# First feed-forward of a two-layer decoder: the scratch of the Hadamard transform laid out by token tile

## The chip, the cores and the metric

The kernel runs on one core of one Trainium2 chip. The metric is the device time of the launch in microseconds (us). Most times below come from one profiled execution, which is described with its own time.

The engines have the names that the profile gives them: PE is TensorE (matrix products, with its weight loads apart as PEld), DVE is VectorE, ACT is ScalarE, POOL is GpSimd, and SP is SyncE, whose queue issues nearly all transfers (DMAs).

## The reference

The program is a decoder of two layers on x of shape (4, 512, 512), four batches of 512 tokens with 512 features. Each layer has a self-attention, a cross-attention and a feed-forward, and each of these six phases ends with `x = layernorm(x + phase(x))`. The change is in the first layer's feed-forward, which works with quantised activations and ternary weights:

```python
def act_quant(x, bits=8):                      # per token
    qb = 128.0
    scale = qb / clip(max(abs(x), axis=-1), 1e-5)
    return clip(round(x * scale), -qb, qb - 1) / scale

def weight_quant(w):                           # ternary
    scale = 1.0 / clip(mean(abs(w)), 1e-5)
    return clip(round(w * scale), -1, 1) / scale

bitlinear = lambda x, w: act_quant(x) @ weight_quant(w).T
gate, up = bitlinear(x, w_gate), bitlinear(x, w_up)       # 512 -> 2048
intermediate = silu(gate) * up
y = bitlinear(fwht(intermediate), w_down)                 # 2048 -> 512
```

`fwht` is the normalised Walsh-Hadamard transform over the 2048 features of a token. It mixes all 2048 features, and the quantisation after it needs the largest magnitude over all 2048 of a token.

## The kernel before

**Phases and lanes.** The phases are called A to F, and each is a Python generator that runs once for each batch: A0 to A3, then B0 to B3, and so on. The first feed-forward is phase C, in `l0_ffn`. The function `lanes` keeps at most two of these tasks alive and advances them in turn, so that C1's first half is recorded between the steps of C0's second half; C2 is alive beside C1's end, and C3 beside C2's second half. Work in the background (loading and quantising weights) is advanced beside them. Inside a task, `Pipe` delays a step by so many ticks. Each engine executes its own instructions in the order that results from this.

**Buffers.** Nearly all tiles are 128 partitions x 2 KB. They come from two pools in SBUF (69 tiles called "o", 13 called "t") and from 8 banks of PSUM.

**Phase C, first half.** Activations are feature-major here: the 512 tokens of the batch lie along a tile's row, 128 features along the partitions. For each of 16 feature tiles o, four products into `pg` (L645) and four into `pu` (L647) give gate and up; DVE, ACT and POOL form silu(gate) * up and split it in two parts (L616 to L624). The transform is factored in two, 2048 = 16 x 128. The factor of 128 is a product with a 128 x 128 matrix `had` over the partitions (L629 and L630, called `ph`). ACT copies the result to a tile `hw` (L635), and SP writes it to a DRAM scratch (L636): 128 rows of 2 KB, one for each feature, in the place o * 128 of a (2048, 512) array. There are two such scratches, used by even and odd batches.

**The way back.** The factor of 16 runs over features that lie in different tiles o. So the scratch is read back (L652) as 16 tiles `z`, tile c holding features i * 128 + c * 8 + b for all 16 i and 8 b, with all 512 tokens in a row. A partition is a pair (i, b), a row is 2 KB, and eight rows that touch stand 256 KB apart from the next eight.

**Phase C, second half.** Now the result is wanted token-major. For each token tile i of 128 tokens and each group g of four, a pass of four products (L713, out `had`, in the profile's name) takes the 128 columns of token tile i out of z tiles 4g to 4g + 3 as weights, against `had16`, and fills a PSUM bank with 512 transformed features of 128 tokens. There are 16 passes for a batch, in the order i = 0, g = 0..3, then i = 1, and so on. A product of f32 appears as two instructions, so a pass is eight of them.

After a pass, `amax` takes the largest magnitude (DVE, L659) and copies the bank out as `q2f` (ACT, L661). After the four passes of a token tile, `scales` forms the scale (L666 to L671), `quant` rounds (ACT L679, DVE L680), `turn` transposes the result back to feature-major by eight products for each half (L686, `q2T`), `flip` copies it (ACT L691), `down` multiplies it with the 16 row tiles of w_down (L699, `dn`), and `add` adds the residual and takes the statistics for the layer norm (L703, L176). In C1 and C3 TensorE's queue holds the passes among transposes and down products of the batch before.

**Weights.** `layout` prepares the inputs on the host, before the launch. It permutes the 2048 rows of w_down to the order in which the passes leave the features.

## Time and profile before

| | before |
|---|---|
| median of 3 runs | 1645.03 us (1643.46 to 1653.15) |
| the profiled execution | 1649.59 us, span 1647.9 us from its first to its last instruction |
| busy: PE, PEld | 1543.2 us (94%), 1106.6 us (67%) |
| busy: DVE, ACT, POOL | 1244.6 us (76%), 1011.3 us (61%), 666.1 us (40%) |
| mean granted clock of TensorE | 0.982 of full |
| bytes moved by DMA | 180.76 MB in 103,237 packets, mean 110 GB/s |
| scratch writes `had_scratch<-hw` | 64, 256 KB each, first issue seen at 481.4 us, last at 723.1 us |
| scratch reads `z<-had_scratch` | 64, 256 KB each, from 518.2 to 737.4 us |

How to read it: phase C takes its place between about 430 and 790 us of the span. A line such as `L713 PE MATMUL had<-had,z ... x512 | 74.0, 289 | 10.5 <-DMA z<-had_scratch 10.2` gives the source line, the engine, the operation, the tile written and the tiles read, the count; then busy time in us and the mean of one in ns; then the idle time of that engine directly before these instructions, and what ended most of it. In the list of transfers the last number is the median time from the issue to the landing. In an order of time, a line gives start, length, engine, line, operation, count, and in brackets the idle time before it with its cause. A waits line gives who waited for whom, us in total, the times, the longest. "Granted clock" is the share of TensorE's full clock that it was given.

### The profile page before, as it was taken

What the parts mean: (1) busy time and instruction counts of PE and PEld (TensorE: products, weight loads), DVE (VectorE), ACT (ScalarE), POOL (GpSimd) and SP (SyncE); (2) the same over time, 40 slices, a digit from 0 to 9 for tenths busy, and PEclk for the clock granted to TensorE, in tenths of its full rate; (3) what the DMA queues carried; (4) which work ended last, traced back from release to release, by engine and by line L of the source; (5) the groups of instructions that cost most, each with busy time, mean ns of one, the idle gap of its engine ahead of it and who ended that gap; (6) DMA issues with size and microseconds to landing.
All of it is one profiled execution on the core that took longest, in us unless ns stands there. A gap on an engine that the chain in (4) does not pass through costs nothing.

```text
span 1647.9 us, 25494 instructions
## 1 busy us (share of the span) xinstructions
PE 1543.2 (94%) x8215; PEld 1106.6 (67%) x8246; DVE 1244.6 (76%) x2684; ACT 1011.3 (61%) x2177; POOL 666.1 (40%) x672
## 2 busy tenths in 40 slices
PE   7999999999999899899999999999998989999995
PEld 5888785444545664467777767777676766686874
DVE  6486589999875678967575666756879899979795
ACT  5333337988777777777696755968543444454542
POOL 6663654556435204420434342342333344333332
PEclk9999999999999999999999999999999999999998
DMA  6043344454125524861433323233445432011000
GB/s 244 29 147 122 122 162 138 133 171 159 52 95 176 186 82 138 245 176 62 130 76 78 78 81 109 69 79 76 154 153 178 142 102 61 24 54 51 1 26 25
DMA packets 103237, 180.76 MB, mean 110 GB/s; under 512 B 16561, under 2 KB 18609, under 8 KB 103105
## 3 DMA queue, kind: packets, MB, share of 16 engines
q1 hardware_dynamic: 98976, 170.69, 33.2%
q0 software_dynamic: 4128, 8.46, 2.1%
q8 instruction: 65, 1.06, 0.3%
q14 instruction: 68, 0.55, 0.1%
HBM read 111.98 MB, written 41.94 MB: 93 GB/s over the span
## 4 chain that ended last, share of the span: by engine, by line
PE 59%; DVE 17%; ACT 9%; DMA 6%; issue 5%; POOL 3%; SPq 1%; DVEq 0%; ACTq 0%; POOLq 0%
PE fg L1104 7%; PE facc L1095 6%; PE dT L881 3%; PE bo L458 2%; ACT de L871 2%; DVE bsm L434 2%; DVE x L200 2%; PE pu L647 2%; PE bT L213 2%; DMA z<-had_scratch 2%; PE pg L645 2%; PE dn L699 2%; PE do L901 2%; PE dq L150 2%; PE bs L486 2%
## 5 line engine op out<-in xcount | busy, mean ns | idle before, releaser
L1068 DVE SCALAR_TENSOR_TENSOR fg<-fg,gs,fg 128x512 f32<-128x512 f32 x220 | 162.3, 744 | 36.5 <-PE fg L1104 17.3
L867 DVE CUSTOM_DVE_ANT_0 de<-ds,negm,thr 128x128 f32<-128x128 f32 (+3 forms) x256 | 126.3, 545 | 34.3 <-PE ds L856 31.2
L1104 PE MATMUL fg<-fxh,gu 128*128 128x512 f32 x352 | 144.2, 410 | 7.6 <-DVE fg L1068 4.6
L871 ACT ACTIVATE de<-de,dm 128x128 f32<-128x128 f32 (+3 forms) x256 | 143.1, 563 | 12.4 <-DVE dm L867 11.9
L1104 PE MATMUL fg<-fxl,gu 128*128 128x512 f32 x352 | 139.1, 395 | 0.0
L442 POOL TENSOR_SCALAR be<-be,bsm 128x512 f32<-128x512 f32 x128 | 95.8, 760 | 104.5 <-DVE bsm L440 74.8
L624 POOL TENSOR_TENSOR hl<-g,hh 128x512 fp32r<-128x512 f32 x64 | 84.1, 1321 | 114.1 <-ACT hh L623 93.4
L1072 POOL TENSOR_TENSOR fg<-fg,fg 128x512 f32<-128x512 f32 x44 | 60.8, 1382 | 128.6 <-ACT fg L1065 89.4
L436 ACT ACTIVATE be<-bs,bsm 128x512 f32<-128x512 f32 x128 | 87.2, 688 | 31.9 <-DVE bsm L434 30.0
L798 POOL TENSOR_TENSOR dql<-dqf,dqh 128x512 fp32r<-128x512 f32 x32 | 41.2, 1289 | 155.1 <-ACT dqh L797 120.9
L881 PE MATMUL dT<-ident,de 128*128 128x128 f32 x640 | 90.3, 279 | 7.6 <-ACT de L871 5.8
L1104 PEld LDWEIGHTS fg<-fxh,gu 128*128 128x128 f32 x352 | 67.1, 191 | 38.1 <-DVE fg L1068 14.2
L881 PEld LDWEIGHTS dT<-ident,de 128*128 128x128 f32 x640 | 72.3, 142 | 26.1 <-ACT de L871 12.7
L1062 ACT ACTIVATE fg<-fg,gs 128x512 f32<-128x512 f32 x88 | 60.4, 686 | 39.9 <-PE fg L1104 39.5
L713 PE MATMUL had<-had,z 128*128 128x128 f32 x512 | 74.0, 289 | 10.5 <-DMA z<-had_scratch 10.2
L434 DVE TENSOR_REDUCE bsm<-bs 128x1 f32<-128x512 f32 x128 | 83.3, 671 | 0.0
L1095 PE MATMUL facc<-p4h,fhh 128*128 128x512 f32 x176 | 71.7, 408 | 8.9 <-DVE fg L1068 6.2
L713 PEld LDWEIGHTS had<-had,z 128*128 128x128 f32 x512 | 66.9, 198 | 18.7 <-DMA z<-had_scratch 7.7
L458 PE MATMUL bo<-bpT,cT 128*64 128x512 f32 x256 | 76.8, 618 | 2.9 <-DVE bpT L449 1.6
L213 PEld LDWEIGHTS bT<-ident,be 128*128 128x128 f32 x512 | 55.0, 141 | 34.1 <-issue 12.3
L213 PE MATMUL bT<-ident,be 128*128 128x128 f32 x512 | 73.2, 281 | 3.8 <-POOL be L442 2.1
L1065 ACT ACTIVATE fg<-fg,gs 128x512 f32<-128x512 f32 x44 | 30.3, 688 | 75.1 <-PE fg L1104 75.1
(332 smaller groups left out, 4676.2 us busy)
## 6 DMA issues: line engine op xcount, KB each, us to landing
x<-x SPq DMA_DIRECT2D x176, 256.0 KB, 3.1
had_scratch<-hw SPq DMA_DIRECT2D x64, 256.0 KB, 2.0
z<-had_scratch SPq DMA_DIRECT2D x64, 256.0 KB, 6.1
stk<-dqh SPq DMA_DIRECT2D x192, 64.0 KB, 2.0
tw<-in_wg_t SPq DMA_DIRECT2D x32, 256.0 KB, 3.7
tw<-in_wu_t SPq DMA_DIRECT2D x32, 256.0 KB, 3.7
tw<-in_wd_t SPq DMA_DIRECT2D x32, 256.0 KB, 2.9
p<-in_gu_p SPq DMA_DIRECT2D x22, 256.0 KB, 2.8
```

The lines of the kernel that those rows point to most:

```text
L213: self.nc.tensor.transpose(pt[:, i * P : (i + 1) * P], srcs[i][:, j * P : (j + 1) * P], self.ident)
L434: nc.vector.tensor_reduce(sm[:, h : h + 1], ps, AX.X, ALU.max, negate=True)
L436: nc.scalar.activation(e, ps, AF.Exp, bias=sm[:, h : h + 1], accum_out=sm[:, 2 + h : 3 + h])
L442: nc.gpsimd.tensor_scalar(es[h][i], es[h][i], sm[:, 4 + h : 5 + h], 1.0, ALU.mult, ALU.mult)
L458: nc.tensor.matmul(po[0][h * 64 : h * 64 + 64, :], cT[j][:, c : c + 64], pTs[h], start=j == 0, stop=j == NT - 1)
L713: nc.tensor.matmul(ps[:, c * P : (c + 1) * P], z[g * 4 + c][:, i * P : (i + 1) * P], self.had16, start=True, stop=True)
L867: nc.vector.tensor_tensor_reduce(es[i], ps, self.negm[:, 384 - P * i :], -1.0, self.thr[:, i : i + 1], ALU.add, ALU.min, n4[:, i : i + 1])
L871: nc.scalar.activation(es[i], es[i], AF.Exp, bias=n4[:, i : i + 1], scale=-1.0, accum_out=den[:, hh * 4 + i : hh * 4 + i + 1])
L881: nc.tensor.transpose(pt[:, o + (i - j) * P : o + (i - j + 1) * P], es[i][:, j * P : (j + 1) * P], self.ident)
L1068: nc.vector.scalar_tensor_tensor(y[u], ps, s, y[u], ALU.mult, ALU.add)
L1095: nc.tensor.matmul(acc[t], h[l][:, c], self.dn[i][r], start=i == 0 and n == 0, stop=i == 10 and n == 2)
L1104: nc.tensor.matmul(ps, self.gu[i, u][:, g * P : (g + 1) * P], xT[g][n], start=n == 0, stop=n == 1)
```

## The change

The scratch keeps the four token tiles apart: its shape becomes (2, 4, 2048, 128) instead of (2, 2048, 512). A write still brings all 512 tokens of 128 features, now as four pieces of 128 tokens (512 B) for each partition, one into each token tile's array. The reads go by token tile i and group g: partition p takes the features 16p to 16p + 15, which are 8 KB in one piece, and tile 4i + g takes four of these features, 2 KB, at a pitch of 8 KB from partition to partition. Pass (i, g) then takes all its four blocks of 128 columns from the one tile 4i + g. A feature f is still i * 128 + c * 8 + b; the partition is now 8i + c // 2, and which features meet in a pass differs, so the rows of w_down are permuted accordingly on the host. The numbers of transfers, bytes and instructions in these steps remain.

```diff
-        self.had_scratch = scratch("had_scratch", (2, 2048, 512))
+        self.had_scratch = scratch("had_scratch", (2, NT, 2048, P))
...
         def keep(o, ph):
             w = self.t("hw")
             nc.scalar.copy(w, ph)
-            pipe.later(2, lambda: nc.sync.dma_start(scratch[o * P : (o + 1) * P, :], w))
+
+            to = scratch[:, o * P : (o + 1) * P, :].rearrange("i p t -> p i t")
+            pipe.later(2, lambda: nc.sync.dma_start(to, w.rearrange("p (i t) -> p i t", i=NT)))
...
-        z = [self.load(self.o("z"), scratch.rearrange("(i c b) t -> c i b t", i=16, c=16)[c]) for c in range(16)]
+        z = [self.load(self.o("z"), scratch[i].rearrange("(p c) t -> p (c t)", c=16)[:, g * 512 : (g + 1) * 512]) for i in range(NT) for g in range(4)]
...
-                    nc.tensor.matmul(ps[:, c * P : (c + 1) * P], z[g * 4 + c][:, i * P : (i + 1) * P], self.had16, start=True, stop=True)
+                    nc.tensor.matmul(ps[:, c * P : (c + 1) * P], z[i * 4 + g][:, c * P : (c + 1) * P], self.had16, start=True, stop=True)
...
-    d["wd_t"] = f["L0_ffn_w_down"].T.reshape(16, 16, 8, 512).transpose(1, 0, 2, 3).reshape(2048, 512)
+    d["wd_t"] = f["L0_ffn_w_down"].T.reshape(16, 8, 16, 512).transpose(2, 0, 1, 3).reshape(2048, 512)
```

## The prediction

> **What bounds the kernel.** I read the page first, then the waits of TensorE around the changed line, then TensorE in order of time in the same places, then the DMA view of short stretches. First the page: the span, the group of the 16-row transform's passes, and the two transfers that the change reshapes.

> ```profile
> span 1647.9 us, 25494 instructions
> ...
> L713 PE MATMUL had<-had,z 128*128 128x128 f32 x512 | 74.0, 289 | 10.5 <-DMA z<-had_scratch 10.2
> ...
> had_scratch<-hw SPq DMA_DIRECT2D x64, 256.0 KB, 2.0
> z<-had_scratch SPq DMA_DIRECT2D x64, 256.0 KB, 6.1
> ```

> TensorE is busy in 94% of the span, so time saved elsewhere counts only where TensorE waits. At L713 it idled 10.5 us in the whole run, 10.2 of them for z tiles on their way from scratch. The first feed-forward runs four times (C0 to C3). Asked in stretches, TensorE's waits for z lie in C1 (563 to 583 us) and in C3 (727 to 746 us):

> ```profile
> PE had L713 <- DMA z<-had_scratch: 6.5, 5, 4.5
> ```

> ```profile
> PE had L713 <- DMA z<-had_scratch: 3.7, 8, 1.3
> ```

> In C0 and C2 there are none: the passes there stand between the gate and up products of the next batch, and the stretches from 518 to 562 us and from 686 to 726 us show TensorE busy throughout. These waits understate the stall, because the weight loads (a pass loads z as weights) have 2.6 and 5.0 us of their own. TensorE in order of time, in C1, shows it (start, length, line, count, idle before):

> ```profile
> 567.76 0.71 PE L713 MATMUL had<-had,z 128*128 128x128 f32 x2 [4.50 <-DMA z<-had_scratch]
> ...
> 576.94 0.49 PE L713 MATMUL had<-had,z 128*128 128x128 f32 x2 [0.44 <-DMA z<-had_scratch]
> 577.92 0.49 PE L713 MATMUL had<-had,z 128*128 128x128 f32 x2 [0.49 <-DMA z<-had_scratch]
> 578.91 0.49 PE L713 MATMUL had<-had,z 128*128 128x128 f32 x2 [0.50 <-DMA z<-had_scratch]
> 579.99 2.30 PE L713 MATMUL had<-had,z 128*128 128x128 f32 x14 [0.59 <-DMA z<-had_scratch]
> ...
> 585.97 0.61 PE L686 MATMUL q2T<-ident,q 128*128 128x128 bf16 x8
> ```

> Two instructions use one z tile, so the starts are the landings: a tile about every 1.0 us. From 568 to 579 us the DMA engines are full and move 267 GB/s, which is 256 KB in 0.98 us. The first four passes need all 16 tiles, the later twelve none. In C3 the same piece of the program lies between these lines:

> ```profile
> 728.84 0.46 PE L713 MATMUL had<-had,z 128*128 128x128 f32 x2 [0.82 <-DMA z<-had_scratch]
> ...
> 749.16 0.61 PE L686 MATMUL q2T<-ident,q 128*128 128x128 bf16 x8
> ```

> What the pieces cost without a wait is read a little later, where all tiles are there: 24 instructions are three passes, then come 16 down products (one record is missing), eight transposes, one pass.

> ```profile
> 758.13 2.90 PE L713 MATMUL had<-had,z 128*128 128x128 f32 x24
> 760.87 3.62 PE L699 MATMUL dn<-tb,q2T 128*128 128x512 bf16 x15
> 764.32 0.61 PE L686 MATMUL q2T<-ident,q 128*128 128x128 bf16 x8
> 764.76 1.11 PE L713 MATMUL had<-had,z 128*128 128x128 f32 x8
> ```

> From start to start: three passes 2.74 us, 16 down products 3.45, eight transposes 0.44, one pass 0.95.

> **The change, part by part.** *Passes and tiles.* TensorE's instructions stay the same in number and kind. In the built program pass n of a batch (n from 0 to 15) uses tile n alone and waits for that one DMA. TensorE's order differs only in C1 and C3, where single z instructions no longer stand between the down products. The order is: pass 0, 16 down products of the batch before, eight transposes, pass 1, eight transposes, passes 2, 3 and 4, 16 down products, then the transposes whose start is the last line of the two fences.
> C1: up to 573.85 us the work is that of before (pass 0 and 16 down products, partly at a granted clock of 0.59 in the stretch 568 to 572). Then 0.44 + 0.95 + 0.45 + 2.74 + 3.45 = 8.03, so the transposes start at 581.9 instead of 585.97: 4.1 us gained. The tiles don't hold this up: tile 4 lands at about 567.7 + 4 x 1.0 = 571.7 and pass 4 starts at about 577.5.
> C3: 728.84 + 0.91 + 3.45 + 0.44 + 0.95 + 0.45 + 2.74 + 3.45 = 741.2 instead of 749.16: 7.9 us gained. It is more than in C1 because TensorE there stops for eight tiles and falls to a granted clock of 0.50 in the stretch 740 to 744.
> Together 12.0 us. The waits for each batch's first tile (4.5 and 0.8 us) stay, since it needs all 16 writes in both kernels.
> *Where it goes.* From 582 to 610 us TensorE is busy 27.8 of 28 us, and the work behind it on the other engines comes from these passes, so it moves up as a block; C3's end starts the next phase in the same way. I count it in full.
> *The writes.* 64 writes of 256 KB now go as four pieces of 512 B for each partition instead of one of 2 KB. No write of such pieces stands in the trace. The nearest row by size is the load of the mask (64 KB, 512 B for each partition), seen alone from 1153 to 1157 us:

> ```profile
> q1 hardware_dynamic: 144, 0.07, 6.8%
> ```

> 6.8% of 16 engines x 4 us is 4.35 us, over 144 packets 30 ns each. For the present write, 489 to 493 us has 239 packets at 28.2%: 18.05 us, 76 ns each. One write is 9 packets an engine before (0.68 us) and 33 after: at 30 ns 0.99 us, so +0.3; at the other end, with each piece as dear as a present packet, 33 x 76 = 2.5 us, so +1.8. I take 0.3, by the row of the same size. The issue took 0.32 us; with a third dimension the nearest row is z's own present load, 0.55, so +0.2. No gain is bounded in, as the bytes are the same. On the path lies only the last write of C1 and of C3: 2 x 0.5 = 1.0 us (between 0 and 4). The other writes follow each other by about 2.3 us (16 in 34 us from 481 us), under which 0.99 disappears; at 2.5 they would not.
> [...]
> *The reads.* z is read as rows of 2 KB at a pitch of 8 KB instead of groups of eight rows 256 KB apart. The loads of wg_t and wu_t have this very shape: their median from issue to landing is 3.7 us against 2.9 for wd_t, whose rows touch; two of them, alone in the stretch from 75 to 81 us, begin at some 140 GB/s (1.9 us a tile), a denser row of seven from 106 to 114 us has 225 (1.17 us). Bounds are 0.68, the rate of the present writes, and 1.9; I take 1.0 to 1.17. In C1 a stall would return only above (577.5 - 567.7) / 4 = 2.4 us a tile, in C3 above 2.0. z's issue becomes plain, 0.33 us like wg_t's instead of 0.55; it is hidden, since the engines are full.
> *The rest* costs nothing: w_down's rows are permuted before the launch and its loads have the same shape; a few quantising steps on VectorE move by some places between instructions that wait for the same passes; no queue is passed by anything, and SP issues the same transfers in the same order.
> Sum: 12.0 - 1.0 = 11.0 us. The profiled execution took 1649.59 us (span 1647.9), which gives 1638.6; it stands 4.6 us above the median of 1645.03 (three runs, 1643.46 to 1653.15), so I predict 1645.0 - 11.0 = 1634 us.

> **The rivals.** *Part of the gain is swallowed.* VectorE is full, 6.0 of 6 us, from 598 to 604 and from 604 to 610; if it were the bound there, C1's 4.1 us are lost (1638), with C3's as well 1646. Against it: before 598 VectorE has slack (6.2 of 8 us), and its queue is fed by the passes that move.
> *The writes set the pace: slower.* In C0, C1 and C3 writes follow each other by 2.0 to 2.3 us; a write is late from 2.3 / 33 = 70 ns a piece on. At 76 ns (2.5 us a write) C0 loses 40 - 34 = 6 us, C1 15 x 2.5 - 30 = 7.5, C3 14 x 2.5 - 28 = 7, in sum 20, and the tiles of the z loads start so much later: 1634 + 20 = 1654. Each further 10 ns adds about 5 us in a batch, so over 1661.5 from some 80 ns on; at 95 ns, 1680. For it: nothing in the trace writes small pieces to HBM. Against it: 30 ns for the small reads.
> *The reads get slow.* At 1.9 us a tile, 16 tiles occupy the engines 30 us instead of 16 in C0 and C2, and the next batch's writes, queued behind them on SP, come 14 us late. ScalarE already waits 2.9 us for such a write at 536 us. If 4 us have cover, 20 of 28 come back: 1654 at most, about 1640 at 1.17.
> *It doesn't do what it says.* The z tiles would still be late for their passes and nothing moves, 1645. The order of the program speaks against it.
> *More than the stall.* If also the first tiles come sooner, at most 4.5 + 0.8 = 5.3 us and the 1.0 come on top: 1628.

> **How the numbers follow.** The forecast gets 0.58 (its own range 1629 to 1640), swallowed 0.12, writes 0.13, slow reads 0.05, nothing 0.04, more 0.08. A measurement of this kernel tells about 1% from no change, that is below 1628.6 or above 1661.5. Faster by over 1%: the forecast's lower edge (0.07) and most of the last rival (0.07), 0.14. Slower: the writes above 80 ns (0.09) and a mixture of both transfers being slow (0.04), 0.13. Within 1%: 0.73. The range runs from 1627, below the last rival, to 1652, which takes in the swallowed gain, no change and milder prices of the two transfers.

> **What would show it.** Right: in C1 and C3 TensorE's wait for z at L713 shrinks to the first tile, about 4.5 and 1 us; the transposes follow the first pass after some 14.1 us in C1 (18.2 before) and 12.4 in C3 (20.3); writes still land in 2 to 2.5 us; from C3's end to the last instruction the length is as before. Wrong: writes that land after 4 us or more, ScalarE or GpSimd waiting for had_scratch, TensorE waiting at L713 in C0 or C2, or the block after 582 us longer than before.

## The result, and the profile after

| | before | after |
|---|---|---|
| median | 1647.18 us (1643.46 to 1653.15, 6 runs) | 1629.21 us (1628.11 to 1630.29, 6 runs) |
| the profiled execution | 1649.59 us, span 1647.9 | 1630.29 us, span 1628.6 |
| mean granted clock of TensorE | 0.982 | 0.987 |

The ratio is 0.9886, with a 95% interval of 0.9872 to 0.9901: the change saves 18.0 us of 1647, between 16.3 and 21.1. The forecast was 11.0 us, so the sign and the range held, but some 7 us of the gain were not foreseen. (The forecast time of 1634 us was off by only 4.8 us, because the median of before, 1645.0 from three runs then, is 2.2 us higher with six.) The question behind the experiments is where those 7 us come from.

The page of after, with the span, the group of the passes and the two transfers (line numbers are two higher than before from L638 on):

```profile
span 1628.6 us, 25543 instructions
...
had_scratch<-hw SPq DMA_DIRECT2D x64, 256.0 KB, 2.4
z<-had_scratch SPq DMA_DIRECT2D x64, 256.0 KB, 5.8
```

The passes no longer stand among the costliest groups of that page. In the longer list of groups their line is this (busy time, mean ns, then idle time before them and its causes):

```profile
L715 PE MATMUL had<-had,z 128*128 128x128 f32 x512 | 66.1, 278 | 2.7 <-DMA z<-had_scratch 1.4 <-ACT q2f L663 1.2
```

The idle time before the passes fell from 10.5 to 2.7 us, and their busy time from 74.0 to 66.1: the same 512 instructions also ran faster. Both remaining waits are those of a first pass. The one that the view puts down to ScalarE (`ACT q2f`), in C3, is a wait for z too: the first tile landed at 721.89 us and the pass began at 722.02. TensorE in order of time, in C1 of after:

```profile
567.08 1.13 PE L715 MATMUL had<-had,z 128*128 128x128 f32 x8 [1.43 <-DMA z<-had_scratch]
568.05 3.62 PE L701 MATMUL dn<-tb,q2T 128*128 128x512 bf16 x15
571.50 0.61 PE L688 MATMUL q2T<-ident,q 128*128 128x128 bf16 x8
571.95 1.11 PE L715 MATMUL had<-had,z 128*128 128x128 f32 x8
572.90 0.61 PE L688 MATMUL q2T<-ident,q 128*128 128x128 bf16 x8
573.34 2.90 PE L715 MATMUL had<-had,z 128*128 128x128 f32 x24
576.08 3.62 PE L701 MATMUL dn<-tb,q2T 128*128 128x512 bf16 x15
579.53 0.61 PE L688 MATMUL q2T<-ident,q 128*128 128x128 bf16 x8
```

The order is the one that the program promised, with no idle time after the first pass: 12.45 us from the first pass to the transposes at the end, against 18.21 before. The wait ahead of it is 1.43 us instead of 4.50. C3, the first and the last line of the same piece, again 12.45 us apart (20.32 before):

```profile
722.02 1.13 PE L715 MATMUL had<-had,z 128*128 128x128 f32 x8 [1.22 <-ACT q2f L663]
...
734.47 0.61 PE L688 MATMUL q2T<-ident,q 128*128 128x128 bf16 x8
```

To see where the time came from, the start of the same TensorE instruction was compared in two traces, at the places named by their time in the first (us, minus is sooner). The last columns use traces from the experiments below.

| place | after against before | after again against before again | reads by token tile, old scratch, against before |
|---|---|---|---|
| 548, ahead of C1's passes | +2.4 | +1.0 | -0.7 |
| 588, behind C1's stall | -6.4 | -7.9 | -7.3 |
| 716, ahead of C3's passes | -7.2 | -8.3 | -8.7 |
| 768, behind C3's stall | -14.7 | -17.0 | -16.8 |
| 980 | -16.2 | -17.0 | -17.8 |
| 1600 | -19.3 | -19.5 | -19.6 |

C1 gives 8.8 us in the first pair (+2.4 to -6.4) and C3 7.5, together 16.3; in the second pair it is 8.9 and 8.7. The forecast had 12.0 for them, less 1.0 for the writes. The rest comes in steps after 768 us: 1.6 us between 960 and 980 in the first pair alone, and in both pairs 1.6 to 2.1 us between 1200 and 1300 and 1.1 us between 1400 and 1500.

### The profile page after: what moved, and what is told of

The parts are those of the page before. It is cut to its first block, busy times and chain, and to the rows that moved or that the text cites. A ratio compares the mean times of both kernels' runs of the same rounds, so it can differ in the third digit from the quotient of the medians.

```text
span 1628.6 us, 25543 instructions
## 1 busy us (share of the span) xinstructions
PE 1532.3 (94%) x8215; PEld 1100.0 (68%) x8246; DVE 1247.6 (77%) x2684; ACT 1010.6 (62%) x2177; POOL 665.9 (41%) x672
## 4 chain that ended last, share of the span: by engine, by line
PE 61%; DVE 17%; ACT 9%; issue 5%; DMA 4%; POOL 3%; SPq 1%; DVEq 0%; ACTq 0%; POOLq 0%
PE fg L1106 7%; PE facc L1097 6%; PE dT L883 3%; PE bo L458 2%; ACT de L873 2%; PE dn L701 2%; PE bT L213 2%; DVE x L200 2%; PE pu L649 2%; PE bs L486 2%; DVE bsm L434 2%; PE pg L647 2%; PE do L903 2%; DVE fg L1070 2%; PE dq L150 2%
## 5 line engine op out<-in xcount | busy, mean ns | idle before, releaser
L1070 DVE SCALAR_TENSOR_TENSOR fg<-fg,gs,fg 128x512 f32<-128x512 f32 x220 | 162.4, 745 | 35.4 <-PE fg L1106 15.2
L873 ACT ACTIVATE de<-de,dm 128x128 f32<-128x128 f32 (+3 forms) x256 | 143.1, 563 | 12.4 <-DVE dm L869 11.9
L312 POOL TENSOR_TENSOR z<-z,rope_cos 128x512 f32<-128x512 f32 x32 | 45.7, 1438 | 73.0 <-DVE zs L310 66.0
L1106 PEld LDWEIGHTS fg<-fxl,gu 128*128 128x128 f32 x352 | 66.8, 190 | 11.9
## 6 DMA issues: line engine op xcount, KB each, us to landing
x<-x SPq DMA_DIRECT2D x176, 256.0 KB, 3.1
had_scratch<-hw SPq DMA_DIRECT2D x64, 256.0 KB, 2.4
z<-had_scratch SPq DMA_DIRECT2D x64, 256.0 KB, 5.8
tw<-in_wg_t SPq DMA_DIRECT2D x32, 256.0 KB, 3.8
tw<-in_wu_t SPq DMA_DIRECT2D x32, 256.0 KB, 3.6
tw<-in_wd_t SPq DMA_DIRECT2D x32, 256.0 KB, 2.9
p<-in_gu_p SPq DMA_DIRECT2D x22, 256.0 KB, 2.7
```

The costliest lines, as they stand in the source:

```text
L873: nc.scalar.activation(es[i], es[i], AF.Exp, bias=n4[:, i : i + 1], scale=-1.0, accum_out=den[:, hh * 4 + i : hh * 4 + i + 1])
L1070: nc.vector.scalar_tensor_tensor(y[u], ps, s, y[u], ALU.mult, ALU.add)
L1106: nc.tensor.matmul(ps, self.gu[i, u][:, g * P : (g + 1) * P], xT[g][n], start=n == 0, stop=n == 1)
```

## The experiments

Nine runs followed, seven of them of changed kernels. The theory after the result was: the passes' order removes the stall as forecast, and the rest is a first tile that comes sooner in C1, and stretches in which TensorE's granted clock is halved.

**Before, unchanged, for a second profile.** 

> The kernel before, unchanged, for a second profile. Theory (the changed kernel gains in C1 and C3 alone, and what the two profiled executions differ by after 800 us is where the granted clock happened to fall): a ratio of 1.000 within 0.003; TensorE waits for z in C1 and C3 again, after the first tile at a pace of about 1.0 us a tile; the last write of C1 lands in 2 to 2.5 us instead of the 3.95 us of the first profile, so the first wait of C1 is about 2.5 us instead of 4.5; the stretches of halved clock near 960, 1292 and 1412 us are not all there again. Rival (the later 4.6 us belong to the change): the same stretches have the same halved clock again, and the distance from C3's end to the last instruction is again longer than in the changed kernel by 4 to 5 us.

Measured: 1650.14 us, ratio 1.0017 (1.0002 to 1.0032). The first tile of C1 was again waited for 4.5 us, so that wait is not an accident of one profile. Stretches of low clock after 800 us lay partly at other places: the one at 960 us was missing, another at 1261 us was new. The interval leaves out 1 although the kernel is the same, so differences of some 0.2% between kernels are not read as effects below.

**The order undone.** The new scratch and its transfers stay, and the order of the passes too, but the loads are issued group by group, with token tile 0 last in each. So the first pass needs the fourth tile, the second the eighth, and the fourth all 16, in the manner of before:

```diff
-        z = [self.load(self.o("z"), scratch[i].rearrange("(p c) t -> p (c t)", c=16)[:, g * 512 : (g + 1) * 512]) for i in range(NT) for g in range(4)]
+        zs = {(i, g): self.load(self.o("z"), scratch[i].rearrange("(p c) t -> p (c t)", c=16)[:, g * 512 : (g + 1) * 512]) for g in range(4) for i in (1, 2, 3, 0)}
+        z = [zs[i, g] for i in range(NT) for g in range(4)]
```

> The changed kernel with the same scratch, the same transfers and the same order on TensorE; only the 16 loads of a batch are issued in another order (by group, token tile 0 last in each group), so that pass g of the first token tile waits for load 4(g+1), as in the kernel before. Theory (the gain is the order of consumption, and the faster reads have a share): with the changed kernel's landings (0.67 us a tile, the last 15.2 us after the first issue) pass 0 waits 2 to 2.8 us more and pass 3 for the 16th load; C1 and C3 each give back 4 to 5 us: 1638 (1635 to 1641), ratio to before 0.992 to 0.996. Rival 1 (the transfers alone made the gain): no difference to the changed kernel, 1629, ratio 0.989. Rival 2 (the order alone made it, the reads have no share): all comes back, ratio 0.998 to 1.002.

Measured: 1643.26 us, ratio 0.9967 (0.9951 to 0.9984), where 1638 was expected. It saves 4.9 us of 1648.16, so some 13 of the 18 us are gone with the order alone, more than was expected. In the traces, what is left of the gain is 4.1 us in C1 and 1.9 in C3. TensorE's waits between 480 and 800 us in this kernel:

```profile
PE had L716 <- DMA z<-had_scratch: 5.8, 3, 3.5
PE had L716 <- ACT q2f L664: 4.5, 1, 4.5
```

The wait of 4.5 us, in C3, is put down to ScalarE, but the fourth tile, which that pass needs, landed at 727.45 us and the pass began at 727.59: it is a wait for z as well. Behind the long idle time the clock was 0.50 in the stretch 728 to 732 us.

**The order alone, with the old scratch.** Scratch and writes of 2-KB rows are those of before; the reads take one token tile and one group each, as four pieces of 512 B for a partition, and one tile feeds one pass:

```diff
-        z = [self.load(self.o("z"), scratch.rearrange("(i c b) t -> c i b t", i=16, c=16)[c]) for c in range(16)]
+        z = [self.load(self.o("z").rearrange("p (c t) -> p c t", c=4), scratch.rearrange("(p c) t -> p c t", c=16)[:, g * 4 : g * 4 + 4, i * P : (i + 1) * P]).rearrange("p c t -> p (c t)") for i in range(NT) for g in range(4)]
```

> The scratch and the writes of the kernel before (2 KB in one piece for each partition), but each z tile is read for one token tile and one group, as four pieces of 512 B for each partition, in the order of the passes. Theory (one tile per pass is what matters): at 30 ns a piece, as in the mask's load, a tile takes 1.0 us, under the 2.0 us at which passes would wait; the gain of the changed kernel comes whole, 1629 within 3, ratio 0.987 to 0.991, and the writes land in 2.0 us. Rival (the fast reads of the new layout are needed): a tile takes over 2 us, the passes wait again in C1 and C3 and the writes behind the loads in C0 and C2 come late: ratio 0.995 or more.

Measured: 1633.21 us (4 runs), ratio 0.9905 (0.9879 to 0.9932), which overlaps the interval of after. With the queue full, tiles land every 0.8 to 0.95 us here, against 0.65 to 0.7 in after, writes land in 2.0 us, and TensorE waits for z only twice between 480 and 800 us:

```profile
PE had L714 <- DMA z<-had_scratch: 2.7, 2, 2.1
```

So the order alone, without the new scratch, brings 15.0 us of 1648.16, most of the gain. Whether the 3.3 to 4.0 us between this median and the two medians of after are real, these four runs don't settle.

**Before, with 4 KB and with 64 KB of padding.** With the queue full, the old reads ran at 256 to 271 GB/s in C1 and C3 (up to 303 in C0), the new ones at 368 to 395. The suspected cause was the 256-KB pitch between the eight-row runs of a read. Behind each block of 128 rows 2 unused rows are left, or 32 (160 in the place of 130):

```diff
-        self.had_scratch = scratch("had_scratch", (2, 2048, 512))
+        self.had_scratch = scratch("had_scratch", (2, 16 * 130, 512))
...
-            pipe.later(2, lambda: nc.sync.dma_start(scratch[o * P : (o + 1) * P, :], w))
+            pipe.later(2, lambda: nc.sync.dma_start(scratch[o * 130 : o * 130 + P, :], w))
...
-        z = [self.load(self.o("z"), scratch.rearrange("(i c b) t -> c i b t", i=16, c=16)[c]) for c in range(16)]
+        z = [self.load(self.o("z"), scratch.rearrange("(i r) t -> i r t", i=16)[:, c * 8 : c * 8 + 8, :]) for c in range(16)]
```

> The kernel before with two empty rows (4 KB) after each block of 128 rows in the scratch, so that the groups of eight rows that one read takes stand 260 KB apart instead of 256 KB; order and sizes as before. Theory (the reads were slow, 265 GB/s, because of the pitch of 256 KB): a tile lands every 0.65 to 0.7 us, the 16th 4 to 5 us sooner, and with the old order C1 and C3 each gain 2 to 4 us: ratio 0.995 to 0.998. Rival (the pitch has nothing to do with it): 1.0 us a tile and a ratio of 1.000 within 0.002.

> The kernel before, with 64 KB of unused scratch behind each block of 128 rows, so that the eight-row runs which the 16 DMA engines read at once lie 320 KB apart instead of 256 (260 KB apart brought the tiles from 0.97 to about 0.9 us). Passes, order and writes stay. Theory A (what slows the old reads is that their rows lie at a pitch that is a power of two): the tiles land every 0.65 to 0.7 us, ScalarE's wait for the first write of C1, behind the reads of C0, falls from 2.9 us to about 1, the stalls of C1 and C3 shrink by a third or more (the last of 16 tiles lands 4 to 5 us sooner), and the time by 3 to 8 us: 1641 to 1646 beside 1649. Theory B (it is the grouping, eight touching rows for each engine, or something else): 0.85 to 1.0 us a tile, ScalarE waits 2.5 us or more, 1646 to 1650.

Measured: ratios 0.9992 (0.9976 to 1.0009) and 1.0005 (0.9991 to 1.0019). The median time from one tile to the next in a batch was 0.84 to 1.01 us with padding. In the four profiles with the old reads and no padding it was 0.85 to 1.04. So no effect of the pitch stands out from this spread, and the time of the kernel didn't move; the theory that it is the main cause fell. With 4 KB of padding the reads ran at 295 GB/s from 572 to 576 us, against 264 without. Why groups of eight touching rows are read more slowly than rows at a pitch of 8 KB stays open.

**After, unchanged, for a second profile.** 

> The kernel after, unchanged, for a second profile and more runs. My theory: the gain beyond the forecast of 11 us has two parts. In C1, the first tile comes sooner, because the last write of C1 no longer shares a DMA engine with a 16-KB packet of TensorE's program code (560.99 us, 1.68 us long, in the profile of before), and TensorE's granted clock doesn't fall to 0.5 for 3.41 us after the shorter wait: 1.9 + 1.7 us. The rest, some 4.6 us after 760 us, is stretches of 3.41 us at clock 0.5 after waits of about 2 us, which come and go from run to run. So: again 1628 to 1632 us, ratio 0.987 to 0.990, first tile of C1 waited for 1.2 to 1.8 us, P0 to the transposes 12.4 to 12.5 us in C1 and C3, the sum of low-clock stretches before 800 us as in the first profile, after 800 us different by one or two stretches. Rival (the new order also shortens something after C3): the same stretches of low clock as in the first profile of after, at the same places.

Measured: 1629.92 us, ratio 0.9895 (0.9869 to 0.9921). The first tiles of C1 and C3 were waited for 1.24 and 1.04 us. Neither of the two low-clock stretches of the first profile between 500 and 800 us (at 508 and 678 us) appeared again. After 800 us there were five instead of four.

**The program code moved, in before and in after.** A DMA view of before, from 560 to 564 us, shows C1's last write (issued at 560.19 and landed at 564.14, which is 3.95 us, where a write that nothing delays takes 2.0). The second line is the rate in 40 slices of 0.1 us:

```profile
DMA  0000000009799899720000000010101000010000
GB/s 0 0 0 0 0 0 0 0 0 164 266 430 348 328 348 410 266 62 0 0 0 0 0 0 0 0 20 0 20 0 20 0 20 20 20 41 0 0 0 0
DMA packets 145, 0.28 MB, mean 70 GB/s; under 512 B 16, under 2 KB 16, under 8 KB 144
## 3 DMA queue, kind: packets, MB, share of 16 engines
q1 hardware_dynamic: 144, 0.26, 18.0%
q8 instruction: 1, 0.02, 2.6%
```

Fifteen sixteenths of the write are through at 561.8 us. Then nothing moves for 0.8 us, and eight single packets of 2 KB (20 GB/s in a slice) follow. In the same stretch lies one packet of the queue "instruction", 16 KB, taken for TensorE's program: the page of before has 65 such packets and 16,461 instructions of TensorE (8215 products and 8246 weight loads), about 253 for a packet. This packet took 2.6% of 16 engines x 4 us = 1.7 us. This looks as if one DMA engine brought that packet first and its share of the write afterwards. To test this, 64 small products stand ahead of TensorE's first one. With their weight loads they are 128 instructions, so they should move all later code packets by half a packet, an estimate from the 253:

```diff
                 ps = self.pa("qk")
+                if b == 0 and w == 0 and m == 0:
+                    for _ in range(64):
+                        nc.tensor.matmul(ps[:, 0:P], self.ident16, self.ident16, start=True, stop=True)
```

> The kernel before with 64 small TensorE products ahead of its first one (128 columns, overwritten), which move all later packets of TensorE's program code by half a packet. My theory (the code packet held up C1's last write): that write lands in 2.0 us instead of 3.9, the wait for C1's first tile falls from 4.5 to about 2.6 us, and the time by 1.9 us, by 3.6 if the clock stays up: 1644.5 to 1646.3 beside 1648.2. The start costs up to 1 us. Rival (the write is late by its place, behind the other writes or its own layout): still 3.9 us, 4.5 us, no change, 1648 to 1649.

> The kernel after with the same 64 products at the start. By the count of instructions the code packet of 571.1 us then comes at about 561.5 us, where C1's last write is moving. My theory: that write lands after 3.5 to 4 us instead of 2.27, C1's first tile is waited for 3.0 to 3.5 us instead of 1.43, and the time rises by 1.6 us, by 3.3 if the clock falls too: 1631 to 1633. Rival: the write stays at 2.27 and the wait at 1.4, 1629 to 1630.

Measured in before: the code packet came at 558.04 us, C1's last write landed after 1.98 us, and the wait ahead of its first pass was 2.60 us. In all five profiles with before's passes and the code in its old place a packet met that write, and it took 3.82 to 3.95 us. The write's cause is thereby shown. But the time, 1648.07 us, ratio 0.9997 (0.998 to 1.0015), didn't move. Two things stand against the gain. The added products cost time themselves: TensorE was some 2.3 us later than in before at 500 us already, and 3.6 us later when it came to C1's passes, and in after the median with these products was 2.3 us longer. And in this profile the sooner first tile did bring C1's last tile 1.7 us sooner after TensorE had come to its passes (15.0 us instead of 16.7), but then the clock was halved from 580.6 to 587.4 us, and from that tile to the transposes TensorE took 7.98 us instead of 5.98. So it left the passes 3.9 us later than in before. What a sooner first tile is worth with the order of before is therefore not shown.

In after the test missed: the code packets came at 554.69 and 574.67 us, not on the last write, which landed in 2.27 us, and the wait was 0.72 us (1632.23 us, ratio 0.991, 0.9888 to 0.9932). That the time lies in the expected 1631 to 1633 us has another reason than the expected one. What a late last write would cost in after was not measured.

**TensorE kept busy ahead of C1, in before.** Thirteen products fill 3 us of the wait ahead of the first pass:

```diff
                 ps = self.pb("had2")
+                if b == 1 and i == 0 and g == 0:
+                    for _ in range(13):
+                        nc.tensor.matmul(ps, self.ident16, tern["wd_t"][0, 0], start=True, stop=True)
```

> The kernel before with 13 products of 512 columns (about 3 us of TensorE's time, overwritten) ahead of C1's first pass, where TensorE waits 4.5 us for the first tile. My theory (the low clock from 568 to 572 us follows the idle time): the wait shrinks to about 1.4 us, the clock stays 1.00 in that stretch, the first pass and its 16 down products take 4.4 us instead of 6.1, and the transposes after the second down group come up to 1.7 us sooner, less where the tiles set the pace; time 1646.5 to 1648 beside 1648.2. Rival (the clock falls for another reason, such as the kind of work): 0.5 again in that stretch, no change.

Measured: 1647.84 us, ratio 1.0002 (0.9986 to 1.0018). The wait fell to 1.50 us as expected, but the clock fell nevertheless, one stretch later (the view by stretches: stretch, its length, busy time of TensorE, granted clock, DMA share, GB/s):

```profile
569.20:572.60 3.40, 1.42 (x8) 1.00 0.94 253
572.60:579.40 6.80, 6.49 (x18) 0.50 1.05 301
```

In the stretch from 569.2 to 572.6 TensorE was busy 1.42 us of 3.4, with the end of the filling and short pieces of passes between waits for tiles. The next 6.8 us ran at half clock. The low clock therefore doesn't hang on the one long wait alone, as the theory had it: it came with the stall here too, though its idle time was divided.

## Why the prediction was right, and where it was short

**The stall: right, in place and size.** For C3 7.9 us were forecast for this part, and 20.32 - 12.45 = 7.87 were measured. For C1 4.1 were forecast and 18.21 - 12.45 = 5.76 measured. The difference is the clock: the step "up to 573.85 us the work is that of before" carried over the stretch at 0.59, and with the stall gone TensorE kept its full clock there, 1.65 us. (In C3 the forecast had counted the slow stretch as a part of the gain, in C1 it had not.) In the second pair the two pieces were 7.32 us shorter in C3 and 5.63 in C1. The view by stretches has it. First before (stretch, its length, busy time of TensorE, granted clock, DMA share, GB/s):

```profile
568.00:572.00 4.00, 3.78 (x14) 0.59 1.00 271
```

The same stretch of after, and C3's whole piece of after, where TensorE is busy all the time at full clock:

```profile
568.00:572.00 4.00, 3.95 (x26) 1.00 0.99 309
...
722.00:734.50 12.50, 12.37 (x87) 1.00 0.85 292
```

**"The waits for each batch's first tile stay": wrong in C1.** 4.50 us became 1.43, and 1.24 in the second profile. Three terms make up the 3.07: C1's last write took 2.27 us instead of 3.95 (1.68), because the program code, moved by the other order of instructions, no longer met it; ScalarE wrote the `hw` tiles 1.73 us sooner in relation to TensorE; the first read took 0.35 longer (3.77 instead of 3.42). In the second pair they are 1.60 and 1.34, and the first read was 0.33 shorter. The first of these is luck of the layout of the code, though it came in every profile with before's passes except the one in which the code was moved.

**"The reads ... 1.0 to 1.17 us a tile", hidden: mis-sized, and not hidden.** With the queue full they take 0.65 to 0.7, the lower bound. The prediction named ScalarE's wait of 2.9 us at 536 us for a write queued behind these reads, but only as a danger if the reads became slower. It is also where faster reads pay. ScalarE's waits from 515 to 550 us, first in before:

```profile
ACT hw L635 <- DMA had_scratch<-hw: 2.9, 1, 2.9
```

The same wait in after:

```profile
ACT hw L635 <- DMA had_scratch<-hw: 0.7, 1, 0.7
```

Those 2.2 us move all later writes of C1, and so its first tile (TensorE itself gained 0.4 us there, so 1.73 are left in relation to it). The other runs agree: in the kernel with the order undone, which has the same fast reads, that wait is 0.4 us, and ScalarE gains 2.4 us on before between 530 and 540 us; in the one with the old scratch, whose reads are slow, it is 2.5 us. Without the order the whole kernel gained some 5 us.

**The writes: right in size, and nearly free.** Those that nothing delays land in 2.26 to 2.30 us (+0.28, forecast +0.3), and their issue takes 0.36 us (+0.04, forecast +0.2). In C3 the first pass waits 1.22 or 1.04 us, against 0.82 in the first profile of before and 2.41 in the second, so this wait can't show the price. In C1 the 0.28 is part of the 2.27 above. The rival that the writes set the pace falls with the same number.

**"I count it in full": right.** From 588 to 716 us the lead of C1 stays (-6.4 to -7.2), and from 768 to 940 it is constant within 0.1 us (-14.7). VectorE took nothing of it, so the swallowed gain falls.

**"From C3's end to the last instruction as before": not quite.** That block was 4.6 us shorter in the first pair of profiles and 2.5 in the second. This does not need the change: against the first profile of before it is 1.8 to 4.6 us shorter in the four kernels with after's order, but also 2.5 to 4.7 us in the four with before's order whose code or scratch was moved or whose wait was filled. The trace's record of the granted clock goes with it. Between 800 and 1600 us it shows 7 and 8 units of 3.41 us at 0.5 in the two profiles of before and 8 in the kernel with the order undone, 4 to 6 in the four just named, and 4 or 5 in those with after's order. A unit costs up to 1.7 us, an estimate from half of 3.41 (the products of 512 columns started every 0.43 us in the unit at 1411 us of before, every 0.23 at full clock ahead of it). Most units follow a wait of 1.9 to 3.4 us that both kernels have.

Whether such a wait is followed by a unit goes with the place where it falls. In every run all slow stretches start whole multiples of 3.413 us apart by the trace's record of the clock (in before, counted from the one at 567.83 us, the next four start 35, 50, 115 and 193 of them later, at 687.30, 738.50, 960.36 and 1226.60 us). The time between can be cut from these starts into windows of that length. The same wait of 1.92 us lies within one such window in before and is cut by a boundary in after (the view by stretches, first before, then after):

```profile
1407.51:1410.92 3.41, 1.49 (x7) 1.00 0.00 0
1410.92:1414.33 3.41, 3.41 (x10) 0.50 0.00 0
...
1388.38:1391.79 3.41, 1.74 (x7) 1.00 0.00 0
1391.79:1395.20 3.41, 3.04 (x13) 1.00 0.02 5
```

Counted in the eleven traces, without their first and last 40 us or so, half clock followed 39 of 39 windows at full clock in which TensorE was busy for less than 0.42 of the window, 30 of 39 with 0.42 to 0.45, 8 of 101 with 0.45 to 0.65, and none of 4736 with more. The first profiles of before and after alone have 6 of 6, 8 of 8, 1 of 21 and none of 857. A wait of 4.5 us leaves at most 1.16 us (0.34) of some window busy wherever it falls, so by these counts the 1.65 us of C1 belong to the stall. A wait of 1.9 us leaves 0.44 at the least, and by these counts its price goes by its place among the windows. So the 2.5 to 4.6 us are for the most part not the change's own; whether a part is lasting is not settled.

The sum: 12.0 of stall as forecast (4.1 and 7.9), 1.65 of clock and 3.07 of first tile in C1, less some 0.4 in C3, give 16.3, and 0.8 between the two and 4.6 after them, which may be luck, make 21.7. The start lost 2.4 (1.1 before 500 us, 1.7 in one slow stretch at 508, 0.4 back at 540), which leaves 19.3 in the profiles, 18.0 in the medians. Of the rivals, "more than the stall" (1628) named the term that was missing, a first tile that comes sooner, and gave it a chance of 0.08.

## What to carry to other kernels

When transfers feed short steps in order, cut them so that each one completes what a single step needs; here that order alone gave 15 us, the new layout with its faster reads alone some 5, and both together 18. A wait that a change makes shorter is priced with what follows it, the clock of the next few microseconds included (1.65 us in C1). A queue that mixes reads and writes couples both ways: the wait that was listed as a danger if the reads got slower was a gain when they got faster (2.9 us in before, 0.7 in after).
